# A graph layer's turned table: built from normalised pieces in the set-up or from reloaded rows in the main loop

## The chip, the cores and the metric

The kernel runs on one core of a Trainium2 chip. The metric is the device time of one execution in microseconds (us), the median of several runs. A core has TensorE (PE: matmuls and transposes, with the load of weights listed apart as PEld), VectorE (DVE), ScalarE (ACT), GpSimd (POOL, which here only issues gathers) and SyncE (SP, which here only issues transfers), each with an instruction queue that it runs strictly in order.

## What is computed

A layer of a graph network over 12,500 nodes of 128 features and 200,000 edges, sorted by their destination `dst`:

```python
h = jnp.maximum(_layernorm(x, axis=-1), 0.0)          # 12500 x 128
agg = segment_sum(h[src], dst, 12500) / jnp.maximum(deg, 1.0)[:, None]
z = jax.nn.relu(agg @ Wg + h @ Ws + bg)               # 128 -> 128
z = jnp.tanh(z @ W1 + b1)                             # 128 -> 512
z = jnp.tanh(z @ W2 + b2)                             # 512 -> 512
return x + (z @ W3 + b3)                              # 512 -> 128
```

All is f32. `src` is drawn at random, so the rows `h[src]` lie anywhere in the table of `h`.

## The kernel before

**Set-up.** x comes in eleven pieces (4, 6, then ten tiles of 128 nodes each, the last one shorter). For each, `centre` sums on VectorE, subtracts the mean, squares on ScalarE and sums again; `factors` takes Sqrt on ScalarE and a reciprocal on VectorE; `scale` writes the normalised piece `h` (L241), which SP stores into `htab`, a table in DRAM. Between the first pieces and behind the last one the edge indices are turned onto partitions by TensorE (`idx_f`, copied by VectorE). POOL gathers the rows of 80 "raw" chunks straight from x at this time (L179); these are normalised later, on VectorE, in the main loop (`centre(ed, ...)`, `raw_scaled`).

**Main loop.** The edges are cut into 1563 chunks of 128. For each chunk, 128 rows of h (one an edge) are multiplied on TensorE with a one-hot matrix `oh` of its destinations (24 columns; made by VectorE, L495, for 8 chunks at once), which adds the rows into the sums of a block of 512 nodes in PSUM: `agg` for chunks inside a block, `edge` for those that reach over its end. There are 25 blocks, smaller ones at the end. The rows of a chunk come in one of four ways:

- gathered: POOL issues one indirect transfer from `htab` (`gather`, L388) into one of AHEAD = 24 row buffers; 1323 chunks in the kernel before;
- lane 0: SP issues 128 transfers of 512 bytes (`row_loads`, tile `srows`); 14 chunks;
- lane 1: ScalarE copies 128 columns out of `tab` (`column_copies`, L442); 50 chunks;
- lane 2: VectorE takes them as 64 pairs (`column_pairs`, L451); 96 chunks.

`tab` is the turned table, 128 features on the partitions x 12,544 nodes, in SBUF. A chunk of lane 1 or 2 gathers columns and is turned back into rows on TensorE (`turn`): one transpose for lane 1, two products (`ident`, `minus`) for lane 2, then a copy `turned` on ScalarE (L476). Columns and row loads are spread by `load_times` over the chunks ahead of their use: one step of a lane's spacing, plus a margin of some 18 to 26 chunks.

**Which chunk takes which way.** `slots` are the chunks 3, 7, 11, ... from FROM to UNTIL that are not raw. A running debt for each way (`owed`) gives each slot to the lane, or to the gather, that is owed most; the counts are SHARES = 14, 50, 96 of 339 slots.

**How the table comes about.** In the main loop, `own(s)` has SP reload four tiles (256 KB) of `htab` into one of two buffers `xb` (shared with the rows of x for the output), and `own_turned(s)` transposes them on TensorE (L381) into `pt`, the one PSUM buffer of `ps_t`, from which ScalarE copies them into `tab` (L476). Three reloads and one transposition stand ahead of chunk 0, the others at the odd chunks up to 49. The two lists run in program order with everything else on these engines.

**The layers behind the sums.** When a block's last chunk is LEAD = 16 chunks past, a list of parts (`mean` on VectorE: sums times reciprocal degree, `mT`; `part0`: `ws` times `tab` and `wg` times `mT`; `part1` to `part3`: the 512-wide layers with their activations on ScalarE, `h`, L473; `part4`: transposes into `pt` and the output add `o` on VectorE, L805) is worked off, one step at each even chunk (`go_on`). From chunk QUICK = 1312 on a planner places the steps instead, by `there`, a due time worked out from a chunk's number among the gathered ones (1.251 us each). Degrees are counted on VectorE every 14 chunks (`nearby`, L535) and turned on TensorE (`degs`, `rd`).

So the order on each engine is that of the loop. TensorE meets chunk after chunk, the parts of the layers between them; VectorE has columns, one-hots, means, output adds and, up to chunk 104 or so, the statistics of the raw chunks; ScalarE has columns, activations and copies.

Of the kernel before, what the change touches and what calls it, by code (L numbers as in the profile page):

```python
# [22 lines left out]
F32 = mybir.dt.float32  # L23
# [8 lines left out]
P = 128  # L32
EPS = 1e-5
CPR = 16
BLK = 512
# [9 lines left out]
SPREAD = 8  # L45
EVERY = 4
AT = 3
SHARES = 14, 50, 96
FROM, UNTIL = 104, 1540
SBUFS = 4  # L50
MARGIN = 18
TOGETHER = 4
# [25 lines left out]
def windowed(ctx, tc, x, src, dst, Wg, Ws, bg, W1, b1, W2, b2, W3, b3, out, flag):  # L78
    nc = tc.nc
    N, D = x.shape  # L80
# [18 lines left out]
    def raw(c):  # L99
        return RAW0 <= c < RAW1 and (c - RAW0) % STEP < GRP  # L100
# [23 lines left out]

    lanes = ([], [], [])
    slots = [c for c in range(AT, NCH, EVERY) if FROM <= c < UNTIL and not raw(c)]
    owed = [0.5 * n for n in SHARES] + [0.5 * (len(slots) - sum(SHARES))]
    for c in slots:
        owed = [o + n for o, n in zip(owed, [*SHARES, len(slots) - sum(SHARES)])]
        kind = max(range(4), key=lambda k: owed[k])  # L130
        owed[kind] -= len(slots)
        if kind < 3:
            lanes[kind].append(c)
    apart = sum(lanes, [])

    blocks, n = [], 0
# [16 lines left out]
    ps_t = ctx.enter_context(tc.tile_pool(name="ps_t", bufs=1, space=PSUM))  # L153
# [22 lines left out]
    for g in range(NRAW):  # L176
        t = raws.tile([P, GRP, D], F32, name=f"raw{g}")
# [7 lines left out]
    ident = const.tile([P, P], F32, name="ident")  # L185
# [5 lines left out]
    lane = shared[:, :W_MAX]  # L191
# [8 lines left out]
    htab = dram.tile([NP, D], F32, name="htab")  # L200
    bytes_at = dram.tile([ahead_of + NROW * ROW + past_end], U8, name="bytes_at")
    tab = const.tile([P, NP], F32, name="tab")
# [33 lines left out]
    def factors(stats):  # L236
        nc.scalar.activation(stats[:, 1], stats[:, 1], AF.Sqrt, bias=eps, scale=1.0 / D)
        nc.vector.reciprocal(stats[:, 1], stats[:, 1])

    def scale(h, xt, k, stats):  # L240
        nc.vector.scalar_tensor_tensor(h, xt, 0.0, spread(stats[:, 1], k), op0=ALU.max, op1=ALU.mult)  # L241

    with tc.tile_pool(name="ln", bufs=2) as ln:
# [53 lines left out]


        pieces = [(0, 4), (4, PIECE - 4)] + [(t, min(PIECE, NT - t)) for t in range(PIECE, NT, PIECE)]
        for i, (t0, k) in enumerate(pieces):  # L300
            xt = ln.tile([P, PIECE, D], F32, name="xt", bufs=3)
            whole = min(N - t0 * P, k * P) // P
            rest = min(N - t0 * P, k * P) - whole * P
            if rest:
                nc.vector.memset(xt[:, whole, :], 0.0)
            nc.sync.dma_start(xt[:, :whole, :], x[t0 * P : (t0 + whole) * P, :].rearrange("(t p) d -> p t d", p=P))
            if rest:
                nc.sync.dma_start(xt[:rest, whole, :], x[(t0 + whole) * P : N, :])
            if i == 1:
                indices("src", src, 0, keep_src)  # L310
            stats = ps_a.tile([P, BLK], F32, name="agg")[:, : 2 * k].rearrange("p (s t) -> p s t", s=2)
            xt = xt[:, :k]
            centre(ln, xt, k, stats)
            factors(stats)
            h = ln.tile([P, PIECE, D], F32, name="h", bufs=2)
            scale(h[:, :k], xt, k, stats)
            nc.sync.dma_start(htab[t0 * P : (t0 + k) * P, :].rearrange("(t p) d -> p t d", p=P), h[:, :k])


        number = sp.tile([NROW, CPR], F32, name="number")  # L320
# [50 lines left out]
    ml = ctx.enter_context(tc.tile_pool(name="ml", bufs=2))  # L371
# [11 lines left out]
    def sp_dma(*a):  # L383
        tc.keep_in_program_order(nc.sync.dma_start(*a))
# [93 lines left out]
    def raw_stats(i):  # L478
        return stats_raw[:, :, i * GRP : (i + 1) * GRP]

    def raw_scaled(i):
        h = raw_rows[i]
        scale(h, h, GRP, raw_stats(i))
        for j in range(GRP):
            rows_t[RAW0 + i * STEP + j] = h[:, j]
# [202 lines left out]
                s = out  # L688
            nc.vector.tensor_tensor(out, s, rd[:, a0 - n : a1 - n], op=ALU.mult)  # L689

    owns, xss, stores = {}, {}, []

    def own(s):

        n0 = s * BLK
        k = -(-min(BLK, N - n0) // P)
        hb = ml.tile([P, BLK // P, D], F32, name="xb")
        sp_dma(hb[:, :k], htab[n0 : n0 + k * P, :].rearrange("(t p) d -> p t d", p=P))
        owns[s] = hb

    def own_turned(s):

        k = -(-min(BLK, N - s * BLK) // P)
        hb = owns.pop(s)
        pt = ps_t.tile([P, BLK // P, P], F32, name="pt")
        for t in range(k):
            pe.transpose(pt[:, t, :], hb[:, t, :], ident)
        act.copy(tab[:, s * BLK : s * BLK + k * P], pt[:, :k, :].rearrange("p t n -> p (t n)"))

    def own_part(b):  # L710

# [121 lines left out]
    def load_times(lane):  # L833
        use = [sum(o < c for o in order) for c in lanes[lane]]
        if not use:
            return
        step = (use[-1] - use[0]) // max(1, len(use) - 1)
        use = [max(FROM - 46 + MARGIN, use[0] - step), *use] if lane else [use[0] - step * k for k in range(SBUFS - 1, 0, -1)] + use
        if lane == 0:
            use = [max(u, FROM // 2 + 7 * step // 8 * i) for i, u in enumerate(use)]  # L840
        some = LOADS[2] if lane == 2 else TOGETHER
        for i in range(len(lanes[lane])):
            for k in range(P // some):
                yield max(1, use[i] + (use[i + 1] - use[i]) * k * some // P - (0, MARGIN, MARGIN + GRP)[lane])
# [9 lines left out]
    def store(upto):  # L854
        while stores and stores[0][0] <= upto:
            sp_dma(*stores.pop(0)[1:])
# [11 lines left out]
            if w[1] is None:  # L868
                work.remove(w)

    nown = -(-N // BLK)
    own(0)
    own(1)
    own_turned(0)
    own(2)
    onehot(0)
    onehot(1)
    told_begins()
# [3 lines left out]
    for c in range(NCH):  # L882
        g = c // GRP
        at = c
        store(c if c >= QUICK else c - LATE)
        if c % GRP == 0 and g + 2 < ngrp:
            onehot(g + 2)
            if raw((g + 2) * GRP):
                raw_scaled(((g + 2) * GRP - RAW0) // STEP)
            if g == 2 + NRAW + 2:  # L890
                worst = checked()
            if 2 <= g < 2 + NRAW:
                centre(ed, raw_rows[g - 2], GRP, raw_stats(g - 2), bufs=1)
            if g == 2 + NRAW + 5:
                factors(stats_raw)

        if c % (GRP // 2) == 0 and g + 2 < ngrp:
            copies, times = loading[2]
            while times and times[0] <= behind:
                times.pop(0)  # L900
                next(copies, 0)
        while c % GRP == GRP // 2 and counted < len(blocks) and reach[counted][-1] // GRP <= g + (c >= QUICK):
            count(counted)
            counted += 1
        while nxt < len(order) and nxt < behind + AHEAD:
            gather(order[nxt])
            nxt += 1
        if not raw(c) and c not in apart:
            behind += 1
            for rows_of_lane, times in loading[:2]:  # L910
                while times and times[0] <= behind:
                    times.pop(0)
                    next(rows_of_lane, 0)
            while turns and turns[0][0] <= behind:
                turn(turns.pop(0)[1])
        if c >= QUICK:

            there = 7.5 + 1.251 * (NRAW * GRP + order.index(c)) if c not in apart else 0
            if c == QUICK:
                now = there - SPREAD  # L920
            while soonest() and max(now, soonest()[2]) < there:
                go_on(soonest())
            now = max(now, there) + 0.27
        add(c)

        lead = LEAD if c < QUICK else 2
        if done < len(blocks) and (c - lead if across[done] else c) >= reach[done][-1]:
            quick = reach[done][-1] + LEAD >= QUICK

            prev, older = (i if i >= 0 and reach[i][-1] + LEAD < QUICK else None for i in (done - 1, done - 2))  # L930
            older = None if quick and prev is None else older
            work.append([layers(done, prev, older), 0, 0, 0, quick and blocks[done][1] <= P])
            done += 1

        if c % TILE_EVERY == 1 and c // TILE_EVERY < NT:
            tallied(c // TILE_EVERY)
            if c // TILE_EVERY == NT - 1:
                outside(worst)
            if c // TILE_EVERY + EARLY < NT:
                seen(c // TILE_EVERY + EARLY)  # L940
        if c % 2 == 1 and c // 2 + 1 < nown:
            own_turned(c // 2 + 1)
            if c // 2 + 3 < nown:
                own(c // 2 + 3)
        if c < QUICK:
            if c % 2 == 0:
                go_on(work[0] if work else None)
        if c == QUICK:
            for b, (_, n) in enumerate(blocks):
                if n < BLK:  # L950
                    own_part(b)
# [376 lines left out]
```

## Time and profile before

| | |
|---|---|
| median of 3 runs | 2171.02 us (2165.9, 2171.02, 2172.37) |
| the profiled execution | 2164.96 us; its span 2163.2 us, mean granted TensorE clock 0.75 |
| TensorE (PE) | 1474.7 us busy, 68% of the span |
| VectorE (DVE) | 1274.1 us, 59% |
| ScalarE (ACT) | 933.4 us, 43% |
| GpSimd (POOL) | 1335.4 us, 62% |
| transfers | 139.16 MB, 64 GB/s on the mean |

A row of the list of groups reads: line, engine, operation, output <- inputs with shapes, count; then busy us and the mean of one in ns; then the engine's idle time just ahead of these instructions, with what ended most of it. A row of the waits reads: engine, what waited and its line <- what ended the wait; then us in all, the number of waits, the longest. A row of the timeline reads: start, duration, engine, line, instruction; in brackets the idle time before it and its releaser. "issue" is time in which nothing that the profile shows was waited for, "remote" is a transfer or a queue that the trace does not name. L378, L381, L473 and L476 are the lines of small helpers that record matmuls, transposes, activations and copies in program order, so the tiles tell their instructions apart.

### The profile page before, as it was taken

What the parts mean: (1) busy time and instruction counts of PE and PEld (TensorE: products, weight loads), DVE (VectorE), ACT (ScalarE), POOL (GpSimd) and SP (SyncE); (2) the same over time, 40 slices, a digit from 0 to 9 for tenths busy, and PEclk for the clock granted to TensorE, in tenths of its full rate; (3) what the DMA queues carried; (4) which work ended last, traced back from release to release, by engine and by line L of the source; (5) the groups of instructions that cost most, each with busy time, mean ns of one, the idle gap of its engine ahead of it and who ended that gap; (6) DMA issues with size and microseconds to landing.
All of it is one profiled execution on the core that took longest, in us unless ns stands there. A gap on an engine that the chain in (4) does not pass through costs nothing.

```text
span 2163.2 us, 34925 instructions
## 1 busy us (share of the span) xinstructions
PE 1474.7 (68%) x5402; PEld 981.4 (45%) x5402; DVE 1274.1 (59%) x7014; ACT 933.4 (43%) x6907; POOL 1335.4 (62%) x1411
## 2 busy tenths in 40 slices
PE   0025543768687787776885876767787687798587
PEld 0024433445454454454553544545454454454457
DVE  3854365756466675665673765666576476566530
ACT  1201144545544444454544445445454454545432
POOL 7756666566666666666666566666666666666661
PEclk9999985766866766776676776777766776788589
DMA  5934221222221222222222122122222122221210
GB/s 137 243 99 124 58 51 49 52 54 58 54 58 49 61 59 55 54 61 59 52 59 57 49 59 58 51 59 60 51 57 63 47 61 66 53 61 53 56 48 22
DMA packets 132962, 139.16 MB, mean 64 GB/s; under 512 B 31655, under 2 KB 109347, under 8 KB 132536
## 3 DMA queue, kind: packets, MB, share of 16 engines
q0 software_dynamic: 44896, 92.04, 16.7%
q1 hardware_dynamic: 84558, 41.29, 7.1%
q10 hardware_dynamic: 3276, 3.51, 0.6%
q14 instruction: 181, 1.48, 0.2%
q8 instruction: 51, 0.84, 0.2%
HBM read 123.71 MB, written 13.03 MB: 63 GB/s over the span
## 4 chain that ended last, share of the span: by engine, by line
PE 37%; DVE 20%; issue 17%; another core or an unknown queue 11%; ACT 9%; DVEq 2%; DMA 1%; ACTq 1%; SPq 0%
PE pm L378 24%; DVE cols L451 12%; PE agg L378 7%; ACT cols L442 7%; PE edge L378 3%; DVEq L399 2%; ACT h L473 2%; PE pt L381 1%; DVE nearby L535 1%; ACTq L399 1%; PE pm L381 1%; DVE mT L689 1%; DVE oh L495 1%; DVE h L241 1%
## 5 line engine op out<-in xcount | busy, mean ns | idle before, releaser
L388 POOL DMA_INDIRECT rows<-htab,scol x1323 | 1257.7, 951 | 759.7 <-issue 294.0
L451 DVE SCALAR_TENSOR_TENSOR cols<-first_only,tab 128x2 f32<-128x2 f32 x6144 | 913.8, 217 | 404.8 <-issue 394.7
L378 PE MATMUL pm<-h,w 128*128 128x512 f32 (+4 forms) x1344 | 836.1, 724 | 184.1 <-ACT h L473 66.8
L442 ACT COPY cols<-tab 128x1 f32 x6400 | 713.9, 188 | 489.1 <-issue 482.3
L378 PEld LDWEIGHTS agg<-oh,rows 128*128 128x128 f32 x1914 | 420.2, 275 | 285.1 <-issue 269.9
L378 PE MATMUL agg<-oh,rows 128*128 128x24 f32 x1914 | 382.1, 314 | 38.7 <-issue 35.0
L378 PEld LDWEIGHTS pm<-h,w 128*128 128x128 f32 x1344 | 253.7, 237 | 213.7 <-ACT h L473 71.6
L378 PEld LDWEIGHTS edge<-oh,rows 128*128 128x128 f32 x732 | 138.7, 238 | 96.1 <-issue 91.1
L473 ACT ACTIVATE h<-pm,b2c 128x512 f32<-128x512 f32 (+4 forms) x112 | 70.7, 631 | 173.7 <-PE pm L378 57.7
L378 PE MATMUL edge<-oh,rows 128*128 128x24 f32 x732 | 131.3, 286 | 17.6 <-issue 14.0
L805 DVE TENSOR_TENSOR o<-pt,xb 128x512 f32<-128x512 f32 x23 | 15.9, 692 | 203.9 <-remote 83.2
L495 DVE TENSOR_TENSOR oh<-shared,dloc 128x192 f32<-128x192 f32 x186 | 64.8, 350 | 86.2 <-remote 34.1
L473 ACT ACTIVATE h<-pm,b1c 128x512 f32<-128x512 f32 (+4 forms) x112 | 70.1, 631 | 99.5 <-remote 33.6
L476 ACT COPY turned<-pm 128x128 f32<-128x128 f32 x146 | 38.2, 262 | 158.2 <-PE agg L378 60.6
L378 PE MATMUL pm<-ident,cols 128*128 128x128 f32 x192 | 57.9, 394 | 54.8 <-ACT h L473 27.3
L179 POOL DMA_INDIRECT raw<-in_x_dram,rsrc x80 | 76.8, 960 | 25.6 <-issue 24.1
L535 DVE TENSOR_SCALAR_CACHE_REDUCE nearby<-nearby,parity 128x656 uint8<-128x656 uint8 x98 | 87.0, 887 | 6.1 <-issue 6.1
L285 PE MATMUL pm<-ident,idx_f 98*128 98x98 f32 x32 | 6.2, 376 | 108.4 <-DVE idx_f L279 68.5
L378 PEld LDWEIGHTS pm<-ident,cols 128*128 128x128 f32 x192 | 40.9, 257 | 71.3 <-ACT h L473 33.8
L378 PEld LDWEIGHTS agg<-oh,turned 128*128 128x128 f32 x194 | 47.2, 270 | 55.9 <-issue 35.0
L381 PE MATMUL pt<-ident,xb 128*128 128x128 f32 x98 | 27.1, 431 | 61.0 <-issue 32.8
L381 PE MATMUL pm<-ident,degs 128*128 128x128 f32 x99 | 24.9, 374 | 62.9 <-ACT h L473 30.3
(120 smaller groups left out, 808.3 us busy)
## 6 DMA issues: line engine op xcount, KB each, us to landing
srows<-htab SPq DMA_DIRECT2D x1792, 0.5 KB
rows<-htab,scol POOLq DMA_INDIRECT x1323
nearby<-bytes_at SPq DMA_DIRECT2D x98, 82.0 KB
xb<-htab SPq DMA_DIRECT2D x24, 256.0 KB
xb<-in_x_dram SPq DMA_DIRECT2D x23, 256.0 KB
out_dram<-o SPq DMA_DIRECT2D x23, 256.0 KB
xt<-in_x_dram SPq DMA_DIRECT2D x8, 640.0 KB
htab<-h SPq DMA_DIRECT2D x8, 640.0 KB
```

Source lines behind the costliest of these rows:

```text
L179: nc.gpsimd.indirect_dma_start(out=t[:, j, :], out_offset=None, in_=x, in_offset=bass.IndirectOffsetOnAxis(ap=rsrc[:, g, j : j + 1], axis=0),)
L241: nc.vector.scalar_tensor_tensor(h, xt, 0.0, spread(stats[:, 1], k), op0=ALU.max, op1=ALU.mult)
L378: tc.keep_in_program_order(nc.tensor.matmul(*a, **k))
L381: tc.keep_in_program_order(nc.tensor.transpose(*a, **k))
L388: nc.gpsimd.indirect_dma_start(out=r, out_offset=None, in_=htab, in_offset=bass.IndirectOffsetOnAxis(ap=scol[:, c : c + 1], axis=0),)
L399: loads, vs = nc.values_load_multi_w_load_instructions(places[min(lane, 1)][r : r + 1, q // EVERY, p0 : p0 + LOADS[lane]], engines=[kind], ...
L442: tc.keep_in_program_order(nc.scalar.copy(to[:, t : t + 1], of))
L451: last[:] = [tc.keep_in_program_order(nc.vector.scalar_tensor_tensor(to, first_only, a, b.to_broadcast([P, 2]), op0=ALU.mult, op1=ALU.add))]
L473: tc.keep_in_program_order(nc.scalar.activation(*a, **k))
L476: tc.keep_in_program_order(nc.scalar.copy(*a))
L495: newest[:] = [nc.vector.tensor_tensor(oh[:, :k, :w], lane[:, None, :w].to_broadcast([P, k, w]), dloc[:, g * GRP : g * GRP + k][:, :, None ...
L535: done = nc.vector.tensor_scalar(w, w, parity[:, t % 2 : t % 2 + 1], None, op0=ALU.is_equal, op1=ALU.add, accum_out=found[:, t : t + 1])
```

## The change

The table is now made in the set-up. Behind `factors` of each piece, the previous piece's normalised tiles are transposed, four at a time, into `pt` and copied into `tab` by ScalarE (`turned`); the last piece is turned behind the loop. `own`, `own_turned`, their 25 reloads and all their calls in the main loop go. Slots now begin at chunk 24, so the first one is chunk 27; row loads (lane 0) still begin at 104. SHARES are 14, 50 and 106 of now 359 slots, and the rule that deals them out works with fractions of a slot: below chunk 104 it gives no row loads, three columns of ScalarE (chunks 39, 67, 95) and six of VectorE (31, 47, 59, 75, 87, 103); from 104 on 14 row loads, 47 columns of ScalarE and 100 of VectorE. The number of gathers falls from 1323 to 1313. `load_times` loses the lower bound that kept columns behind the reloads.

```diff
--- before.py
+++ after.py
@@ -45,8 +45,8 @@
 SPREAD = 8
 EVERY = 4
 AT = 3
-SHARES = 14, 50, 96
-FROM, UNTIL = 104, 1540
+SHARES = 14, 50, 106
+FROM, UNTIL, ROWS_FROM = 24, 1540, 104
 SBUFS = 4
 MARGIN = 18
 TOGETHER = 4
@@ -124,11 +124,13 @@
 
     lanes = ([], [], [])
     slots = [c for c in range(AT, NCH, EVERY) if FROM <= c < UNTIL and not raw(c)]
-    owed = [0.5 * n for n in SHARES] + [0.5 * (len(slots) - sum(SHARES))]
+    late = sum(c >= ROWS_FROM for c in slots)
+    owed = [0.5] * 4
     for c in slots:
-        owed = [o + n for o, n in zip(owed, [*SHARES, len(slots) - sum(SHARES)])]
+        shares = [SHARES[0] / late * (c >= ROWS_FROM), *(n / len(slots) for n in SHARES[1:])]
+        owed = [o + n for o, n in zip(owed, [*shares, 1 - sum(shares)])]
         kind = max(range(4), key=lambda k: owed[k])
-        owed[kind] -= len(slots)
+        owed[kind] -= 1
         if kind < 3:
             lanes[kind].append(c)
     apart = sum(lanes, [])
@@ -297,6 +299,17 @@
 
 
         pieces = [(0, 4), (4, PIECE - 4)] + [(t, min(PIECE, NT - t)) for t in range(PIECE, NT, PIECE)]
+        def turned(h, t0, k):
+            for s in range(0, k, 4):
+                m = min(4, k - s)
+                pt = ps_t.tile([P, BLK // P, P], F32, name="pt")
+                for t in range(m):
+                    nc.tensor.transpose(pt[:, t, :], h[:, s + t, :], ident)
+                nc.scalar.copy(
+                    tab[:, (t0 + s) * P : (t0 + s + m) * P], pt[:, :m, :].rearrange("p t n -> p (t n)")
+                )
+
+        unturned = []
         for i, (t0, k) in enumerate(pieces):
             xt = ln.tile([P, PIECE, D], F32, name="xt", bufs=3)
             whole = min(N - t0 * P, k * P) // P
@@ -312,9 +325,13 @@
             xt = xt[:, :k]
             centre(ln, xt, k, stats)
             factors(stats)
+            while unturned:
+                turned(*unturned.pop())
             h = ln.tile([P, PIECE, D], F32, name="h", bufs=2)
             scale(h[:, :k], xt, k, stats)
             nc.sync.dma_start(htab[t0 * P : (t0 + k) * P, :].rearrange("(t p) d -> p t d", p=P), h[:, :k])
+            unturned.append((h, t0, k))
+        turned(*unturned.pop())
 
 
         number = sp.tile([NROW, CPR], F32, name="number")
@@ -688,24 +705,7 @@
                 s = out
             nc.vector.tensor_tensor(out, s, rd[:, a0 - n : a1 - n], op=ALU.mult)
 
-    owns, xss, stores = {}, {}, []
-
-    def own(s):
-
-        n0 = s * BLK
-        k = -(-min(BLK, N - n0) // P)
-        hb = ml.tile([P, BLK // P, D], F32, name="xb")
-        sp_dma(hb[:, :k], htab[n0 : n0 + k * P, :].rearrange("(t p) d -> p t d", p=P))
-        owns[s] = hb
-
-    def own_turned(s):
-
-        k = -(-min(BLK, N - s * BLK) // P)
-        hb = owns.pop(s)
-        pt = ps_t.tile([P, BLK // P, P], F32, name="pt")
-        for t in range(k):
-            pe.transpose(pt[:, t, :], hb[:, t, :], ident)
-        act.copy(tab[:, s * BLK : s * BLK + k * P], pt[:, :k, :].rearrange("p t n -> p (t n)"))
+    xss, stores = {}, []
 
     def own_part(b):
 
@@ -835,9 +835,9 @@
         if not use:
             return
         step = (use[-1] - use[0]) // max(1, len(use) - 1)
-        use = [max(FROM - 46 + MARGIN, use[0] - step), *use] if lane else [use[0] - step * k for k in range(SBUFS - 1, 0, -1)] + use
+        use = [use[0] - step, *use] if lane else [use[0] - step * k for k in range(SBUFS - 1, 0, -1)] + use
         if lane == 0:
-            use = [max(u, FROM // 2 + 7 * step // 8 * i) for i, u in enumerate(use)]
+            use = [max(u, ROWS_FROM // 2 + 7 * step // 8 * i) for i, u in enumerate(use)]
         some = LOADS[2] if lane == 2 else TOGETHER
         for i in range(len(lanes[lane])):
             for k in range(P // some):
@@ -868,11 +868,6 @@
             if w[1] is None:
                 work.remove(w)
 
-    nown = -(-N // BLK)
-    own(0)
-    own(1)
-    own_turned(0)
-    own(2)
     onehot(0)
     onehot(1)
     told_begins()
@@ -938,10 +933,6 @@
                 outside(worst)
             if c // TILE_EVERY + EARLY < NT:
                 seen(c // TILE_EVERY + EARLY)
-        if c % 2 == 1 and c // 2 + 1 < nown:
-            own_turned(c // 2 + 1)
-            if c // 2 + 3 < nown:
-                own(c // 2 + 3)
         if c < QUICK:
             if c % 2 == 0:
                 go_on(work[0] if work else None)
```

## The prediction

> **What bounds the kernel now.** I read the page's engine totals and costliest groups first, then the waits (whole span, and by stretch), the busy time per 100 us, the timeline of the set-up and of the first chunks, and the chain that ended last.
>
> ```profile
> span 2163.2 us, 34925 instructions
> L388 POOL DMA_INDIRECT rows<-htab,scol x1323 | 1257.7, 951 | 759.7 <-issue 294.0
> L451 DVE SCALAR_TENSOR_TENSOR cols<-first_only,tab 128x2 f32<-128x2 f32 x6144 | 913.8, 217 | 404.8 <-issue 394.7
> L442 ACT COPY cols<-tab 128x1 f32 x6400 | 713.9, 188 | 489.1 <-issue 482.3
> ...
> POOL rows L388 <- PE agg L378: 168.8, 160, 6.0
> POOL rows L388 <- remote: 154.0, 114, 3.3
> POOL rows L388 <- PE edge L378: 68.8, 67, 4.7
> ```
>
> The gathers on POOL look like the bound (1257.7 us busy) and are not: POOL stood 169 + 154 + 69 = 392 us waiting for one of its 24 row buffers, which TensorE frees. So a gather saved is worth nothing where POOL is already ahead. A chunk that is not gathered costs VectorE (913.8 + 394.7) / 96 = 13.6 us, or ScalarE (713.9 + 482.3) / 50 = 23.9 us. What sets the pace from chunk 112 on is TensorE in its written order and the two engines that it waits for (rows for 305 to 2060 us, the first five from TensorE's waits, the last the group of VectorE's output adds):
>
> ```profile
> PE pm L378 <- ACT h L473: 79.7, 31, 8.2
> PE pm L378 <- ACT turned L476: 44.3, 15, 7.7
> PE pm L381 <- ACT h L473: 43.1, 10, 20.4
> PE pm L381 <- ACT turned L476: 27.6, 7, 11.0
> PE pm L378 <- DVE mT L689: 22.1, 3, 15.8
> ...
> L805 DVE TENSOR_TENSOR o<-pt,xb 128x512 f32<-128x512 f32 x22 | 15.2, 692 | 201.9 <-remote 83.2 <-PE agg L378 64.6 <-PE pm L378 20.1
> ```
>
> TensorE waits for ScalarE (195 us in these four rows alone) and hardly for VectorE (22 us). VectorE itself comes early to the output add of a block and stands there, 202 us over 22 blocks: 9 us of slack a block.
>
> **The change part by part.**
>
> Set-up. Each piece of ten tiles gets ten transposes and three copies on engines that were idle; the question is ScalarE's order, where Square and Sqrt now stand between those copies, with one PSUM buffer for all groups.
>
> ```profile
> 90.03 1.48 DVE L241 SCALAR_TENSOR_TENSOR h<-xt,agg 128x1280 f32<-128x1280 f32 x1
> 96.30 1.27 ACT L231 ACTIVATE sq<-xt 128x1280 f32<-128x1280 f32 x1 [3.02 <-DVE xt L228]
> 97.60 1.50 DVE L234 TENSOR_REDUCE agg<-sq 128x10 f32<-128x1280 f32 x1
> ...
> 128.41 1.09 PE L381 MATMUL pt<-ident,xb 128*128 128x128 f32 x4
> 129.54 0.59 ACT L476 COPY tab<-pt 128x512 f32<-128x512 f32 x1 [1.97 <-PE pt L381]
> 130.56 1.09 PE L381 MATMUL pt<-ident,xb 128*128 128x128 f32 x4
> ```
>
> A group of four takes 130.56 - 128.41 = 2.15 us in this ping-pong, so 4 + 4 + 2 tiles take some 5.5 us. The normalised piece is there at 91.5 and the next Square but one starts at 96.3: 4.8 us. So that Square starts about 0.7 us late, and the reduction that follows its end within 0.03 us starts late with it. Eight pieces at that pace make 6 us at most, 0 where VectorE waits for other things anyway. I take +4 us; the first gather moves by as much. Price without cover: every further microsecond of a group goes 2.6 times per piece onto the set-up.
>
> First stretch (123 us to the second block's mean). Removed: 25 reloads of 256 KB, 98 transposes and 25 copies from the queues of SP, TensorE and ScalarE. They made everything late there: the table was whole only at 223 us, VectorE's first column came at 237 and TensorE stood 15.8 us for a mean that lay behind columns.
>
> ```profile
> 123.20 0.94 POOL L388 DMA_INDIRECT rows<-htab,scol  x1 [19.28 <-DVE degs L510]
> 124.45 0.95 POOL L388 DMA_INDIRECT rows<-htab,scol  x1 [0.30 <-issue]
> 223.38 0.37 ACT L476 COPY tab<-pt 128x256 f32<-128x256 f32 x1 [0.78 <-PE pt L381]
> 237.54 1.19 DVE L451 SCALAR_TENSOR_TENSOR cols<-first_only,tab 128x2 f32<-128x2 f32 x8 [0.25 <-DVE shared L234]
> 239.01 1.14 DVE L451 SCALAR_TENSOR_TENSOR cols<-first_only,tab 128x2 f32<-128x2 f32 x8 [0.28 <-issue]
> 382.50 2.08 PE L378 MATMUL pm<-mT,wg 128*128 128x512 f32 x2 [15.81 <-DVE mT L689]
> ...
> DVE rd L596 <- remote: 23.4, 1, 23.4
> DVE oh L495 <- PE pt L381: 21.0, 1, 21.0
> DVE oh L495 <- remote: 20.3, 2, 12.3
> DVE oh L495 <- PE agg L378: 16.6, 3, 9.2
> DVE oh L495 <- PE edge L378: 3.1, 1, 3.1
> ```
>
> With the table in place TensorE and POOL run at 124.45 - 123.20 = 1.25 us a gather from the start. But VectorE becomes the bound: the lane rule puts six columns of VectorE (chunks 31 to 103) and three of ScalarE (39, 67, 95) ahead of the old first one, and VectorE's queue also holds the statistics of the raw chunks there. Its ledger up to the mean at 382: idle 23.4 + 21.0 + 20.3 + 16.6 + 3.1 = 84 us (last five rows, 123 to 310 us), all of it for TensorE, goes; six columns come, at 11.7 us (8 x 1.46 us, from 237.54 to 239.01) to 13.6 us, 70 to 82 us. So that mean comes 2 to 14 us earlier; I take 8. TensorE reaches chunk 112 some 20 us earlier, but must wait for this mean. The three columns of ScalarE (72 us) have its idle time up to 223 us as cover.
>
> Chunk 104 to the end. Here the lane rule leaves 14 reloaded rows, cuts ScalarE from 50 to 47 columns and raises VectorE from 96 to 100. ScalarE: 3 x 23.9 = 72 us less over 22 blocks, 3.3 us a block. Worth between nothing (it was idle) and 72 us (always waited for); TensorE's wait for ScalarE, 195 us of 1755, is 11% of the time, and 6% fewer columns shorten each wait too: I take -12 us, nearer the low end. VectorE: 4 x 13.6 = 54 us more, 2.5 us a block against 9 us of slack; between nothing and 54; I take +3, since three waits in 22 blocks were for its mean. TensorE: one column of VectorE takes two products where one of ScalarE takes one; four against three, under 5 us and inside its waits: 0. Ten gathers less: 12.5 us on POOL, hidden behind its 392 us of waiting: 0, at most -12 if POOL were the end. SP loses 25 issues ahead of the chunk rows: these only start earlier, 0. The end from chunk 1312 on keeps its order.
>
> Sum: +4 - 8 - 12 + 3 = -13 us. The profiled execution took 2164.96 us (span and 1.8 around it), so 2152; the median of the runs is 2171.02, 6 us above, so 2158 is forecast there.
>
> **The rivals.**
>
> Slower, by stalls in the ping-pong: TensorE and ScalarE hand one PSUM buffer to and fro, and in the trace the hand-over sometimes takes long although nothing is recorded between.
>
> ```profile
> 141.59 1.12 PE L381 MATMUL pt<-ident,xb 128*128 128x128 f32 x4 [4.88 <-issue]
> 159.18 0.59 ACT L476 COPY tab<-pt 128x512 f32<-128x512 f32 x1 [17.64 <-remote]
> 169.71 0.59 ACT L476 COPY tab<-pt 128x512 f32<-128x512 f32 x1 [9.94 <-remote]
> 45.78 0.57 DVE L293 CAST scol<-pm 128x392 int32<-128x392 f32 x1 [6.91 <-remote]
> 56.29 0.57 DVE L293 CAST scol<-pm 128x392 int32<-128x392 f32 x1 [9.94 <-issue]
> L476 ACT COPY tab<-pt 128x512 f32<-128x512 f32 x24 | 14.1, 586 | 91.0 <-remote 49.4 <-issue 16.6 <-PE pt L381 13.5
> ```
>
> The transposes recorded to 142.7 were copied at 159.2. Before, such a stall held up the table alone; in the set-up Square stands behind the copy and VectorE behind Square. For it: the set-up has two of its own (6.9 and 9.9 us, on VectorE's copies of transposed indices). Against: they may belong to the reloads. If half of the 66 us (49.4 + 16.6) falls where VectorE waits, the set-up grows by 33 instead of 4: 2187. It decides from a stall of 17 us in all, which eats the gain.
>
> Slower, by the clock. TensorE would be nearly idle between its bursts in the set-up.
>
> ```profile
> 0.00:100.00 100.00, 3.14 (x16) 2.54 (x16) 61.17 (x83) 16.92 (x21) 74.62 (x85) 1.00 0.72 187
> ```
>
> If its clock were halved there, a group would take 1.1 us longer, a piece some 2.9, eight pieces 23: 2181. The granted clock was 1.00 in this stretch with TensorE 3.14 us busy, which speaks against it. The Trainium skill (TensorE: Matmul & The Clock Gate, The HAM clock gate) says that the default state is throttled to half and that only some 3.4 us of sustained work releases it; by that rule the transposes run at half rate. The row disagrees, as far as it records the clock.
>
> Slower, by VectorE. It was 20.6% of the chain from 1000 to 2060 us.
>
> ```profile
> by line: PE pm L378 21.9%; DVE cols L451 20.6%; issue 17.9%; another core or an unknown queue 9.0%; ACT cols L442 6.7%; PE agg L378 6.4%; DVEq L399 3.7%; PE edge L378 2.6%; DVE nearby L535 1.9%; DVE mT L689 1.4%; ACT h L473 1.2%; ACTq L399
> ```
>
> If half of its 54 us lands on the chain, 27 for 3: 2182. The 202 us of slack speak against it.
>
> Faster still: if TensorE keeps its 20 us at chunk 112 and the relief of ScalarE is worth 20: 2138.
>
> No change: VectorE's fuller first stretch cancels the earlier table: 2165 to 2177. That the change does less than it says can be excluded: table, lanes and loads follow from the code.
>
> **How the numbers follow.** A measurement here tells 0.3% (6.5 us) from no change. Chances: forecast 0.33 (2145 to 2164), faster still 0.15, no change 0.14, stalls 0.22, clock 0.05, VectorE 0.11. So faster 0.48, same 0.14, slower 0.38. Both signs hold much: the forecast's own range is 2145 to 2164, the whole 2128 to 2196, which leaves out the worst stalls and the far end of the gains.
>
> **What would show it.** Right: first gather at 127 us or before, copies of the table within 1 us of their transposes, VectorE without idle time from there to the second mean, that mean at 365 to 380 us, less waiting of TensorE for ScalarE afterwards, and output adds still waiting on VectorE. Wrong: a first gather after 140 us (stalls), a second mean after 385 us (VectorE overfull), waits of TensorE for the mean several times 22 us (VectorE bound), or POOL no longer waiting for buffers.

## The result, and the profile after

The changed kernel took 2229.14 us (median of 4), the kernel before 2168.46: ratio 1.0286, 95% interval 1.0247 to 1.0326. It is slower by 61 us, and the forecast of 2158 us (2128 to 2196) was wrong in direction. One fact is needed to read what follows: the later runs fell on five chips. On three of them (called plain chips here) the kernel before takes 1782.6 to 1784.0 us; on two (called slow-issue chips) 2159.7 and 2190.0 us, like the chip of this comparison. Numbers are compared only between chips of one kind, and with the kernel before on the same chip where a total is judged.

Stages of the spans, by the first product of a chunk on TensorE:

| first comparison | first product | from there to chunk 112 | from there to the end |
|---|---|---|---|
| before | 127.7 us | 177.8 us | 1857.7 us |
| after | 161.5 us | 202.3 us | 1863.1 us |

So 34 us were lost in the set-up, 24 us up to chunk 112, and 5 us in the 1450 chunks behind, where 9 us less were forecast. The page of the profile after, span, gathers and columns:

```profile
span 2226.9 us, 35676 instructions
L405 POOL DMA_INDIRECT rows<-htab,scol x1313 | 1243.4, 947 | 834.2 <-issue 286.2
L468 DVE SCALAR_TENSOR_TENSOR cols<-first_only,tab 128x2 f32<-128x2 f32 x6784 | 1008.4, 218 | 478.2 <-issue 467.2
L459 ACT COPY cols<-tab 128x1 f32 x6400 | 714.5, 188 | 495.4 <-issue 486.6
```

GpSimd lost its ten gathers (14 us busy) and idles 75 us more; VectorE's columns cost 95 us more busy and 73 us more of idle "issue" between them. The loss itself is read in the timeline of the set-up (TensorE's transposes, ScalarE's copies and Squares, VectorE's reduction; the last raw gather on GpSimd):

```profile
61.67 0.69 PE L307 MATMUL pt<-ident,h 128*128 128x128 f32 x2 [9.64 <-issue]
65.94 0.37 ACT L308 COPY tab<-pt 128x256 f32<-128x256 f32 x1 [4.32 <-DMA idx_raw<-in_dst_dram]
66.20 1.27 ACT L233 ACTIVATE sq<-xt 128x1280 f32<-128x1280 f32 x1
66.36 1.11 PE L307 MATMUL pt<-ident,h 128*128 128x128 f32 x4 [4.00 <-issue]
76.44 0.58 ACT L308 COPY tab<-pt 128x512 f32<-128x512 f32 x1 [8.96 <-issue]
76.92 1.27 ACT L233 ACTIVATE sq<-xt 128x1280 f32<-128x1280 f32 x1
78.22 1.50 DVE L236 TENSOR_REDUCE agg<-sq 128x10 f32<-128x1280 f32 x1 [9.22 <-ACT sq L233]
...
103.35 0.94 POOL L181 DMA_INDIRECT raw<-in_x_dram,rsrc  x1 [0.31 <-issue]
...
115.37 1.12 PE L307 MATMUL pt<-ident,h 128*128 128x128 f32 x4 [1.89 <-ACT tab L308]
116.52 0.58 ACT L308 COPY tab<-pt 128x512 f32<-128x512 f32 x1 [0.89 <-PE pt L307]
...
158.87 0.94 POOL L405 DMA_INDIRECT rows<-htab,scol  x1 [54.58 <-DVE degs L527]
```

The transposes recorded from 66.36 to 67.5 were copied at 76.44: 10.1 us from the first transpose to the copy, where 115.37 to 116.52 is 1.15. The Square behind that copy and the reduction behind the Square wait with it, VectorE for 9.2 us. Groups of two take 4.3 and 5.0 us, groups of four 10.1 to 10.8: 2.1 to 2.7 us a transpose, so it is not one fixed hand-over. Seven groups are long, the last of them, begun at 105 us, with 7.1 us; the last raw gather was issued at 103.35, and from 115 on no group is long.

The first stretch, by the columns of VectorE and ScalarE while GpSimd issued its first 42 gathers, and TensorE's first turn of a column:

```profile
185.96 0.22 DVE L468 SCALAR_TENSOR_TENSOR cols<-first_only,tab 128x2 f32<-128x2 f32 x1 [1.19 <-issue]
186.64 0.19 ACT L459 COPY cols<-tab 128x1 f32 x1 [1.20 <-issue]
187.35 0.22 DVE L468 SCALAR_TENSOR_TENSOR cols<-first_only,tab 128x2 f32<-128x2 f32 x1 [1.17 <-issue]
188.05 0.19 ACT L459 COPY cols<-tab 128x1 f32 x1 [1.22 <-issue]
...
216.83 0.77 PE L395 MATMUL pm<-ident,cols 128*128 128x128 f32 x2 [28.78 <-remote]
...
443.42 2.07 PE L395 MATMUL pm<-mT,wg 128*128 128x512 f32 x2 [11.93 <-DVE mT L706]
```

Each engine starts one instruction in 1.4 us, in turn: one every 0.7 us between them. I call this slow issue. It does not set in with the first gather (158.87): up to 172 us VectorE started 35 pairs some 0.13 us apart. In the forecast a pair cost 0.18 us (8 in 1.46); here the first column took from 166.8 to 207.2, and TensorE stood 28.8 us at its turn. On a plain chip the same column, beside the same gathers, comes in bursts of eight as forecast:

```profile
107.90 4.49 DVE L468 SCALAR_TENSOR_TENSOR cols<-first_only,tab 128x2 f32<-128x2 f32 x32
112.64 1.14 DVE L468 SCALAR_TENSOR_TENSOR cols<-first_only,tab 128x2 f32<-128x2 f32 x8 [0.24 <-issue]
114.45 1.14 DVE L468 SCALAR_TENSOR_TENSOR cols<-first_only,tab 128x2 f32<-128x2 f32 x8 [0.68 <-issue]
```

### The profile page after: what moved, and what is told of

Read it like the earlier page. It is cut to its first block, busy times and chain, and to the rows that moved or that the text cites. A ratio compares the mean times of both kernels' runs of the same rounds, so it can differ in the third digit from the quotient of the medians.

```text
span 2226.9 us, 35676 instructions
## 1 busy us (share of the span) xinstructions
PE 1484.5 (67%) x5442; PEld 976.6 (44%) x5442; DVE 1365.2 (61%) x7654; ACT 936.9 (42%) x6921; POOL 1321.2 (59%) x1401
## 5 line engine op out<-in xcount | busy, mean ns | idle before, releaser
L405 POOL DMA_INDIRECT rows<-htab,scol x1313 | 1243.4, 947 | 834.2 <-issue 286.2
L468 DVE SCALAR_TENSOR_TENSOR cols<-first_only,tab 128x2 f32<-128x2 f32 x6784 | 1008.4, 218 | 478.2 <-issue 467.2
L395 PEld LDWEIGHTS agg<-oh,rows 128*128 128x128 f32 x1894 | 399.4, 266 | 298.2 <-issue 242.1
L395 PE MATMUL agg<-oh,rows 128*128 128x24 f32 x1894 | 370.4, 310 | 62.0 <-DVE oh L512 31.6
L395 PEld LDWEIGHTS edge<-oh,rows 128*128 128x128 f32 x732 | 144.0, 244 | 130.0 <-issue 110.4
L395 PE MATMUL pm<-ident,cols 128*128 128x128 f32 x212 | 64.1, 393 | 154.1 <-remote 50.8
L395 PE MATMUL edge<-oh,rows 128*128 128x24 f32 x732 | 136.7, 291 | 43.8 <-issue 27.9
L307 PE MATMUL pt<-ident,h 128*128 128x128 f32 x98 | 28.4, 435 | 119.2 <-issue 70.6
L307 PEld LDWEIGHTS pt<-ident,h 128*128 128x128 f32 x98 | 16.9, 215 | 130.0 <-issue 99.6
L395 PE MATMUL pm<-minus,cols 128*64 128x128 f32 x212 | 59.0, 367 | 4.9 <-issue 4.8
```

Source lines behind the costliest of these rows:

```text
L307: nc.tensor.transpose(pt[:, t, :], h[:, s + t, :], ident)
L395: tc.keep_in_program_order(nc.tensor.matmul(*a, **k))
L405: nc.gpsimd.indirect_dma_start(out=r, out_offset=None, in_=htab, in_offset=bass.IndirectOffsetOnAxis(ap=scol[:, c : c + 1], axis=0),)
L468: last[:] = [tc.keep_in_program_order(nc.vector.scalar_tensor_tensor(to, first_only, a, b.to_broadcast([P, 2]), op0=ALU.mult, op1=ALU.add))]
```

## The experiments

Theory A: beside gathers that GpSimd issues without a break, the small instructions of the other engines start slowly; the transposes of the set-up suffer first. Rivals: the hand-over of the one PSUM buffer; TensorE's clock; the early columns.

**Plain chips: what the parts are worth there.** The first four runs were meant to take the loss apart and met a chip that has none (kernel before 1783.5 us).

`e1_table_only`, table in the set-up, no other lanes:

```diff
-SHARES = 14, 50, 106
-FROM, UNTIL, ROWS_FROM = 24, 1540, 104
+SHARES = 14, 50, 96
+FROM, UNTIL, ROWS_FROM = 104, 1540, 104
```

> The changed kernel with its table built in the set-up, but columns only from chunk 104 on (14, 50, 96), as before. Theory A (slow issue: while GpSimd issues gathers without a break, the other engines start about one instruction every 0.7 us between them, which hits the transposes of the set-up and the early columns): the set-up stays long, first product of a chunk at 158 to 164 us, and the rest gives back some of it because the reloads are gone, so 2180 to 2205 us. Theory B (the 34 us of the set-up are all; the early columns cost nothing): the same time as the changed kernel, 2220 to 2235 us. Theory C (the early columns cost all): 2160 to 2175 us.

Measured: 1782.1 us, ratio 0.9994 (0.9984 to 1.0004). The table in the set-up costs and gains nothing there. First product at 110.0 us.

`e2_no_raw` (changed kernel) and `e3_before_no_raw` (kernel before) leave out the raw gathers; the rows of these chunks are ones, so their part of the sums is missing:

```diff
-        for j in range(GRP):
-            nc.gpsimd.indirect_dma_start(
...
+        nc.gpsimd.memset(t, 1.0)
```

> The changed kernel without the 80 raw gathers of the set-up: these rows are ones instead, set by GpSimd. Theory A (slow issue beside gathers): no group of four transposes takes more than 2 us from its first transpose to its copy, and the first product comes 40 us or more earlier than 161.5 us, at 110 to 120 us. Rival (hand-over of the one PSUM buffer): groups of 10 us remain between 50 and 112 us, first product after 145 us. Rival (TensorE's clock is low because it is idle): it is as idle here, so groups stay slow too.

> The kernel before without the 80 raw gathers (ones instead). Theory A: the copies of the turned source indices, which came 6.9 and 9.9 us late, follow their transposes within 1 us, and the first product comes at 105 to 115 us instead of 127.7. Rivals (hand-over, clock): the two waits stay, first product after 122 us.

Measured: first products at 98.8 and 96.2 us, totals 1762.9 and 1767.3 (one run each). They tell nothing for or against A, since on this chip no group is long with the raw gathers either; `e2` was run again on a slow-issue chip, below.

`e4_three_psum`, `pt` from the pool of three buffers:

```diff
-                pt = ps_t.tile([P, BLK // P, P], F32, name="pt")
+                pt = ps_m.tile([P, BLK // P, P], F32, name="pm")
```

> The changed kernel with the set-up's transposes in the pool of three PSUM buffers instead of the one of ps_t. Theory A: TensorE itself is slow, a group of four still needs some 10 us while raw gathers are issued; first product at 150 to 165 us and 2210 to 2235 us in all. Rival (hand-over of one buffer): groups overlap, first product at 125 to 138 us, 2190 to 2205 us in all.

Measured: 1776.05 us (one run), first product at 108.7. Inconclusive for the same reason.

`e5_after` and `e6_before`, both kernels unaltered, on another plain chip:

> The changed kernel, unaltered, on the chip of the last experiments, where the kernel before took 1783.5 us instead of 2168.5 and no stretch of 0.7 us an instruction shows. Theory A (the loss of 60 us comes from that slow issue alone): no loss here; GpSimd issues without a break, so ten gathers less at 1.25 us are a gain of up to 12 us, 1770 to 1780 us. Rival (the set-up's transposes or the early columns cost by themselves): 1815 to 1850 us.

> The kernel before, unaltered, for its trace on this chip. Theory A: transposes of the source indices are copied within 1 us (6.9 and 9.9 us late in the first trace), the transposed groups of the table too, GpSimd never waits for long and no column stream falls to 0.7 us an instruction; 1780 to 1786 us.

Measured: 1773.99 against 1782.6 us, ratio 0.9949 (0.9933 to 0.9966); `e6` 1784.7 (one run). The change is a gain of 8.6 us there. The rows of the page (the engine in 40 slices, then the gathers), before and after, and in the trace of before the copies of turned indices:

```profile
POOL 7777777777777777777777777777777777777774
L388 POOL DMA_INDIRECT rows<-htab,scol x1323 | 1254.9, 949 | 403.4 <-issue 202.8
...
29.95 2.12 DVE L293 CAST scol<-pm 128x392 int32<-128x392 f32 x4
```

```profile
POOL 7777777677777777777777777777777777777774
L405 POOL DMA_INDIRECT rows<-htab,scol x1313 | 1243.6, 947 | 406.0 <-issue 207.0
```

GpSimd never stops: it is the bound on a plain chip, at 1.25 us a gather. The four copies of indices come back to back; in the first trace the last two came 6.9 and 9.9 us late. The main loop's turns of the reloaded tiles, which waited up to 17.64 us for their copies in the first trace, are all copied within 1.2 us of their first transpose in `e6`, with the same one PSUM buffer. So the kernel before had the slow issue too in its first trace; that this makes up all of the 385 us between the two kinds of chip was not shown.

`e7_ten_less` (kernel before, only `SHARES = 14, 50, 106`), `e10_late_columns` (changed kernel, only `FROM = 104`) and `e9_twenty_less` (changed kernel, only `SHARES = 14, 60, 116`), on a third plain chip:

> The kernel before with 106 chunks on VectorE instead of 96, from chunk 104 on, the table still by reloads: ten gathers less and nothing else of the change. Where GpSimd issues without a break, theory A (the gathers are the bound there): 10 x 1.25 us less, 1768 to 1774 us against 1782.6. Rival (the gain of the changed kernel comes from the table in the set-up): 1780 to 1785 us. If this run shows the slow issue (kernel before at 2165 us): the gathers are not the bound, and VectorE's ten columns cost 0 to 40 us more, 2165 to 2205 us.

> The changed kernel with its 50 and 106 columns from chunk 104 on only: the table in the set-up and ten gathers less, but no early columns. Where GpSimd issues without a break: early columns cost nothing, the same 1772 to 1776 us as the changed kernel. If this run shows the slow issue: 20 to 40 us less than the changed kernel, 2190 to 2210 us, as its first columns no longer share the slow issue with GpSimd's first long run of gathers.

> The changed kernel with 60 chunks on ScalarE and 116 on VectorE: twenty gathers less than the changed kernel, to see whether the bound moves on. Where GpSimd issues without a break: up to 25 us less than 1774, 1749 to 1760 us; if VectorE or TensorE takes over, 1760 to 1775 us. If this run shows the slow issue: slower than the changed kernel, 2230 to 2290 us.

Measured against 1784.0 us: `e7` 1772.4, ratio 0.9934 (0.9916 to 0.9952); `e10` 1770.2, 0.9926 (0.9907 to 0.9944); `e9` 1769.5, 0.9924 (0.9908 to 0.9941). The gain on a plain chip is that of ten gathers alone (12.5 us): `e7` has it without the table. Twenty gathers fewer still (`e9` has 1293) bring 1 to 3 us, not 25: in `e9` GpSimd's last gather starts at 1740 us instead of 1751 (`e7`, `e10`), and the end does not follow even that. TensorE's waits for means, of `e9` and then of `e10`, point to what took over, VectorE with its 116 columns (`e5`, which has the early columns as `e9` has, waits 24.8 us):

```profile
PE pm L395 <- DVE mT L706: 90.1, 21, 16.2
```

```profile
PE pm L395 <- DVE mT L706: 13.1, 5, 5.8
```

`e8_hold` (kernel before, the raw gathers from the 17th on behind a copy of `scol` on VectorE):

> The kernel before, whose raw gathers from the 17th on wait until the source indices are turned (some 32 us), so that GpSimd pauses while TensorE transposes. With GpSimd as the bound: its pause of some 7 us is lost, 1786 to 1792 us. If this run shows the slow issue: the two waits of 6.9 and 9.9 us for turned indices go, first product 10 us or more earlier than 127.7, and 2150 to 2165 us in all.

Measured 1783.0 us, ratio 0.9995. The 17th gather was still issued at 23.2 us, so the pause did not come about, and the run says nothing on it.

**Imitating the two losses on the plain chip of `e7`.** In `e11_slow_transposes` and `e12_slow_column` the slow parts are made by hand:

```diff
+                for _ in range(12 if 4 <= t0 < 3 * PIECE else 1):
...
```

```diff
-                for p, to, a, b in two(2, c, p0):
+                for p, to, a, b in [x for x in two(2, c, p0) for _ in range(4 if c == lanes[2][0] else 1)]:
```

> The changed kernel, in which each group of transposes of the second to the fourth piece is issued twelve times over, so that a group of four takes some 10 us, as it did in the first trace between 50 and 112 us. Theory A (these slow groups, by way of ScalarE's queue, made the set-up longer by 34 us): the first product comes 25 to 40 us later than 109.9 us, at 135 to 150 us, and where GpSimd issues without a break all of it is added to the end, 1798 to 1815 us. Rival (the groups were slow, but the set-up waited for something else, such as the transfers): first product before 120 us, under 1785 us.

> The changed kernel, in which every pair of VectorE's first column (chunk 31) is issued four times over, some 50 us for the column as in the first trace. Theory A (a late early column holds TensorE up, and what it costs in the end depends on whether GpSimd's 24 buffers cover it): TensorE reaches chunk 112 20 to 35 us later than at 260.9 us; the total is 0 to 15 us more than 1774 where GpSimd's buffers cover the wait. Rival (VectorE has slack there): chunk 112 within 8 us of 260.9 and the same total.

Measured (one run each): `e11`, with groups of four of 5.5 to 8.6 us instead of 10, first product at 120.9 us, 11 later than in `e5`, total 1785.9, 12 more. The delay was smaller than expected, and the groups were shorter than meant; that the copies hold up the set-up and all of it reaches the end is borne out. `e12`: the column took 89 us, TensorE stood 63 us, reached chunk 112 at 317.3 instead of 260.9, total 1828.5, 54 more. The total missed what was expected (0 to 15): GpSimd's 24 buffers covered next to nothing. Its idle time ahead of the gathers is 463 us on the page, against 406 in `e5`, and this makes up the 54 us.

**On slow-issue chips.** The next runs met one (kernel before 2190.0 us, one run).

`e13_slower_transposes` is `e11` with 24 for 12, `e14_column_twice` is `e12` with 2 for 4, `e15_late_again` is `e10` again:

> The changed kernel with each group of transposes of the second to the fourth piece issued 24 times over: groups of four of about 10 us, the length of the first trace (twelve times gave 5.5 us and a first product 11 us later). Theory A (the length of these groups is the 34 us of the set-up): first product 28 to 45 us after 109.9 us, 138 to 155 us, and all of that in the total, 1802 to 1820 us. Rival (something else made up two thirds of the 34): first product before 130 us, total under 1796 us.

> The changed kernel with VectorE's first column (chunk 31) issued twice over, some 30 us for it against 11 (four times took 89 us, held TensorE up for 63 us and cost 54). Theory A (GpSimd runs up to 24 gathers ahead, 30 us; only what is later than that is lost): chunk 112 reached 10 to 20 us later than at 260.9 us, but the total within 6 us of 1774. Rival (every microsecond of a late early column is lost): total 1784 to 1794 us.

> The changed kernel without early columns once more, for a chip with the slow issue: there 20 to 40 us less than the changed kernel, 2190 to 2210 us, with the first product still near 161 us. On a chip without it the same 1770 us as before, which tells nothing new.

Measured (one run each): `e15`, with no early columns, 2251.5 us, 61.5 more than before on that chip, first product at 164.3 us, chunk 112 190.9 us later. So the early columns are not the cause of the loss, although in the first trace TensorE stands 29 us for one. `e14` 2272.3: more than `e15`, but the imitation adds to a column that is slow already, so it decides nothing. `e13`, whose numbers were meant for a plain chip, started its first product at 225.2 us, 60.9 later than `e15`, and took 2317.9, 66 more: set-up time passes to the end on this kind of chip as well (`e13` has early columns, `e15` has not). Its first long group, 96 transposes in a row, shows the slow issue on TensorE itself:

```profile
45.34 6.60 PE L308 MATMUL pt<-ident,h 128*128 128x128 f32 x34 [13.90 <-issue]
...
100.32 0.37 PE L308 MATMUL pt<-ident,h 128*128 128x128 f32 x1 [2.43 <-issue]
103.12 0.37 PE L308 MATMUL pt<-ident,h 128*128 128x128 f32 x1 [2.43 <-issue]
...
114.32 6.48 PE L308 MATMUL pt<-ident,h 128*128 128x128 f32 x36 [0.33 <-issue]
121.48 5.46 PE L308 MATMUL pt<-ident,h 128*128 128x128 f32 x48 [0.68 <-ACT tab L309]
```

The first 34 start some 0.2 us apart, then one starts every 2 to 3 us until 109 us (the last raw gather starts at 102.6), and from 114 us on the old pace is back. In the short groups of the other traces the recorded starts lie 0.21 to 0.27 us apart and only the copy is late, so there the trace does not tell a slow transpose from a late word of its end. No buffer changes hands inside this group, so it cannot be waiting for a hand-over. VectorE and ScalarE start nothing from 60 to 110 us. A transpose is a weight load and a matmul, so at 2.8 us a transpose TensorE alone starts one instruction in 1.4 us; the 0.7 us seen between two engines is therefore not a limit that they share.

The last three ran on another slow-issue chip (kernel before 2159.65 us, one run): `e16_twenty_more` is the kernel before with `SHARES = 14, 50, 76`; `e17_table_only_again` and `e18_no_raw_again` are the kernels of `e1` and `e2`.

> The kernel before with 76 chunks on VectorE instead of 96: twenty more gathers, 1280 fewer small instructions of VectorE. Theory A (on a chip with the slow issue, the number of instructions that run beside GpSimd's gathers is what costs, not the gathers): faster there, by 30 to 70 us, 2120 to 2160 us against 2190. Rival (GpSimd's gathers bound the kernel on both kinds of chip): slower by up to 25 us on both. On a chip without the slow issue both expect 1797 to 1809 us.

> The table in the set-up alone (14, 50, 96, columns from chunk 104), which made no difference on a chip without the slow issue (0.9994). On a chip with it: theory A (the transposes beside raw gathers cost the set-up 34 us, the rest comes from more columns) 2205 to 2235 us against 2190 before; rival (the whole 60 us lies in the table) 2245 to 2255.

> The changed kernel without the 80 raw gathers (their rows are ones). On a chip with the slow issue: theory A, no group of transposes takes longer than 2 us, first product at 98 to 115 us instead of 161.5, the total 45 to 65 us less than the changed kernel; rival (groups are slow there whatever GpSimd does) first product after 145 us. On a chip without it, 98.8 us as before.

Measured (one run each): `e16` 2184.7, slower by 25 us, which is 20 x 1.25 us. Theory A's second half, that instructions and not gathers cost there, falls. `e17` 2228.6, 68.9 more than before: the table in the set-up by itself costs all of the loss. The 8 us beyond it are less than ten gathers and within what single runs differ by (2162.5 to 2172.4 us for the kernel before in the first comparison). `e18` 2169.9, with the first product at 99.7 us instead of `e17`'s 163.0, and 59 us less in all (its lanes are those of the changed kernel). Timelines of `e17`, then of `e18`:

```profile
65.40 1.11 PE L307 MATMUL pt<-ident,h 128*128 128x128 f32 x4 [4.00 <-issue]
75.47 0.58 ACT L308 COPY tab<-pt 128x512 f32<-128x512 f32 x1 [10.13 <-remote]
...
163.01 0.62 PE L395 MATMUL agg<-oh,rows 128*128 128x24 f32 x2 [1.61 <-DMA rows<-htab,scol]
```

```profile
55.22 1.12 PE L303 MATMUL pt<-ident,h 128*128 128x128 f32 x4 [0.67 <-ACT tab L304]
56.37 0.58 ACT L304 COPY tab<-pt 128x512 f32<-128x512 f32 x1 [1.21 <-PE pt L303]
...
99.70 0.62 PE L391 MATMUL agg<-oh,rows 128*128 128x24 f32 x2 [1.93 <-DMA rows<-htab,scol]
```

One chip, the same one PSUM buffer, two set-ups that differ in the raw gathers alone: with raw gathers the groups of four up to 87 us take 10.1 to 10.6 us, without them none takes more than 2.9 (most 1.15; the plain chip of `e5` has some of up to 3.9 too). This shows that the gathers make the groups slow; whether their issuing or their transfers do it was not separated. It also excludes the two rivals: the hand-over is the same in both, and so is TensorE's rate, since transposes start 0.21 to 0.27 us apart in both. The Trainium skill (TensorE: Matmul & The Clock Gate, The HAM clock gate) would have these transposes at half rate in both; the spacing agrees with that (`e13` has 0.11 us from 121 us on), but a factor of two is not the factor of nine seen, and without gathers the groups are not slow.

## Why the prediction was wrong, step by step

**What bounds the kernel.** It was put as TensorE and its waits, with gathers worth nothing. On a plain chip the gathers are the bound (`e7`: ten less, 11.6 us less), and on a slow-issue chip twenty more cost 25 us (`e16`). GpSimd's 392 us of waiting for buffers did not mean that a gather is free: its idle time ahead of the gathers is 764.6 us in `e16` and 759.7 in the first trace of before, so the twenty gathers came on top of it. Why they did, where GpSimd waits, was not settled.

**Set-up, +4 us.** Measured +34 (161.5 against 127.7). This is the step that failed. The chain was right (transposes, copy, Square, reduction), but a group was priced from a row of the main loop, 2.15 us; beside raw gathers it takes 10. The rows that said so stood in the prediction: index copies 6.9 and 9.9 us late in the set-up itself, under the same raw gathers. They were taken as rare stalls. The rival "stalls in the ping-pong" had this loss at 33 us and the mechanism half right: its place and chain, but not the hand-over. The stalls that it showed from the main loop were the slow issue too (`e6` has none). Its 33 us was half of their 66 us, so that it lies close to the measured 34 is luck. Its 2187 us was too low because it kept the other gains.

The rival of the clock was set aside for a wrong reason: the row's 1.00 was read as the full clock. In `e13` the row says 1.00 from 45 to 51 us, where transposes start 0.21 us apart, and 1.00 again from 121 to 150 us, where they start 0.11 us apart; from 114 to 119 us it says 0.50, with 0.21. So transposes 0.21 us apart run at half rate, whatever the row says so early in the trace. Those of the set-up do, and so do those of the main loop from which the price was taken: the half rate was in the price already.

**First stretch, -8 us.** Measured +24.5. VectorE's columns were priced at 11.7 to 13.6 us; the first took 40. The mean of the second block came at 443 us, not 365 to 380 (34 us of this are the set-up's). `e15` and `e17`, without early columns, still lose 13 and 7 us in this stretch against the first trace of before, though the reloads are gone. Their gain shows up to chunk 56 (79 us instead of 100) and is given back by chunk 112 (112 and 106 instead of 78).

**Chunk 104 to the end, -9 us.** Measured +5 behind chunk 112. TensorE's four rows of waiting for ScalarE fell from 195 to 131 us, as forecast (305 to 2060 us):

```profile
PE pm L395 <- issue: 70.3, 49, 7.2
PE pm L395 <- ACT h L490: 60.9, 29, 9.3
PE pm L395 <- ACT turned L493: 51.0, 18, 6.6
PE pm L395 <- remote: 50.6, 16, 10.4
PE pm L395 <- DVE cols L468: 39.4, 5, 11.0
...
PE pm L398 <- remote: 25.1, 5, 10.8
...
PE pm L398 <- issue: 15.7, 3, 10.2
PE pm L398 <- ACT h L490: 12.3, 5, 4.1
...
PE pm L398 <- ACT turned L493: 6.6, 2, 3.9
```

Of the 64 us, 31 came back as "issue" and "remote", which were 131 us before (the four rows that follow) and are 162, and 39 as waits for VectorE's columns, which were 2 before. Three of these five waits, 21 us, still lie ahead of chunk 112; from there on over as long a stretch (364 to 2119 us) the three sums are 139, 166 and 18 us and waits for means are 29 instead of 22, so the reading holds.

```profile
PE pm L378 <- issue: 55.7, 37, 7.1
...
PE pm L378 <- remote: 42.6, 13, 7.2
...
PE pm L381 <- issue: 20.9, 13, 4.4
...
PE pm L381 <- remote: 11.5, 3, 4.9
```

A shorter wait in one row was counted as time gained without asking what would end last next.

**What would show it.** Of the signs named, a first gather after 140 us (158.87) and a second mean after 385 us came, the signs of stalls and of an overfull VectorE. The other two did not: TensorE's wait for the mean was 22.4 us, as before, and GpSimd still waited for buffers.

**Open.** `e17` loses 69 us. Against `e16` on the same chip, whose set-up is that of the kernel before, 37 lie in the set-up (163.0 against 126.3 us) and 7 in the first stretch; by subtraction the other 25 lie behind chunk 112. What costs them there is not known. What makes issue slow on some chips and not on others is not known either. Every timed execution on record comes with a recorded span, some 2 us short of its time; so the times cannot tell whether the recording itself has a part in the slow issue, and no run without it is on record.

## What to carry to other kernels

Price a moved operation from rows of the stage it moves into, not from where it stood: two late index copies of the set-up priced its transposes better than 98 transposes of the main loop. An engine that is idle in a stage is not free there, if what its work is handed to stands on the path. Where chips differ by a fifth, judge an edit on both kinds: this one is 0.5% faster on one and 2.9% slower on the other, and ten gathers less alone (`e7`) have the gain without the table, though `e7` was not run on a slow-issue chip.

## What the runs showed of the hardware

On the chips of the first comparison and of the last two groups of runs, an uninterrupted run of gathers slows the starts of the other engines' small instructions. VectorE's pairs and, in turn with them, ScalarE's copies came 1.4 us apart (after, 178 to 211 us; pairs 0.14 to 0.18 otherwise). TensorE, with the other two at rest, started a transpose every 2.8 us (`e13`); groups of two and four f32 transposes of 128 x 128 reached their copy after 2.1 to 2.7 us a transpose instead of 0.28. Not every instruction is hit: TensorE's products, two a gather, kept pace with the gathers up to 188 us in after, while VectorE and ScalarE were slow. On three other chips none of this shows. A gather itself takes 1.25 us on both. The slow issue sets in late and ends late: 13 us after the first gather in the main loop of after, some 20 to 30 us after the first raw gather in the set-ups, and in the set-up of after it was gone 12 us after the last. The Trainium skill (SBUF — State Buffer, Who interferes with whom) names the port pair that VectorE shares with GpSimd as the one place where engines contend. That rule does not cover what is seen here, since TensorE and ScalarE are slowed as well.
